# Graph attention on one core: the order of the seven block products of a pair of row tiles

## The chip, the core and the metric

The kernel runs on one core of a Trainium2 chip. TensorE (PE) does the matrix products into PSUM banks, VectorE (DVE), ScalarE (ACT) and GpSimd (POOL) do the elementwise work, and SyncE (SP), ACT and POOL issue the DMAs. The metric is the device time of one execution in microseconds (us). All data is float32. [...]

## The reference

```python
def reference(x, adj, W_q, b_q, W_k, b_k, W_v, b_v):   # x 2708 x 1024, adj 2708 x 2708
    h = maximum(layernorm(x, eps=1e-5), 0)
    q = h @ W_q.T + b_q;  k = h @ W_k.T + b_k;  v = h @ W_v.T + b_v
    z = (q @ k.T) / sqrt(1024) * adj
    z = where(z == 0, -10000, z)
    return x + relu(softmax(z, axis=1) @ v)
```

The entries of `adj` are 0 or 1, with about 4 ones in a row (probability 0.0014771 each). So a row attends to a handful of neighbours.

## The kernel before, in words

**What it computes.** The product of the query and key weights is formed once: M = W_q^T W_k with the scale, so that a score is (h_i M + c)·h_j. The rows of `h` go to DRAM (`h_dram`). A search finds up to 16 neighbours of every row. A counting sort orders the rows by their number of neighbours, so that a tile of 128 sorted rows needs only as many slots as its largest row; 21 full tiles are handled in this way, and 20 rows stay over. For every slot of a tile a gather fetches 128 neighbour rows (`g`); DVE multiplies them with the query rows and sums to one score a row (L664), ACT takes the exponential (L680), and DVE forms the weighted sum of the same rows (`weights`, then `sums` with L717). Each sum u is then multiplied by W_v, and relu, x and the scatter to the output follow. A general path at the end (from L1034) runs only for inputs that the sparse path can't handle.

**Seven products for a pair.** Two tiles of rows times a 1024 x 1024 matrix are eight block products of 128 x 512 x 512; `multiply` does them with seven, in the manner of Strassen and Winograd. `blocks` prepares the left operands: transposed quarters a11, a12, a22 (copied from PSUM by ACT) and their sums s1 to s4 (DVE, or partly POOL for the first pairs). `upper` transposes the first tile (8 transposes on PE), `lower` the second and forms the sums. The right operands are M's quarters and four sums of them in T. One block product is `add_block`: four matmuls that accumulate in one bank.

A pair uses three banks. X and Z are seeded with the bias by `banks_for` (two ACT copies), in the pair before. Y is a copy of X made by ACT (L789). In `multiply` the order is: X += a11·M00; Y = copy of X; Z += s1·T0; p5 = copy of Z; Y += s2·T1; u2 = copy of Y; X += a12·M10, and X is the first result c11; Y += s3·T2, then c22 = Y + p5 on DVE; Z += s4·M11, then c12 = Z + u2 on DVE; Y += a22·T3 and Y is the last result c21. A bank can be added to again only when its copy or sum has been read: Y·s3 waits for u2, Y·a22 for c22, Z·s4 for p5. Below, "Y·a22" means the product that adds a22·T3 to Y.

After each product `after(i)` with i from 0 to 6 runs other parts of the program: the next pair's `upper` at i = 0 and `lower` at i = 2 (for pair FIRST - 1 at 3 and 5), its bank seeds at 3, row loads, steps of the search, and a share of the attention.

**The units.** There are 20 units: ten query pairs (`q`, multiplied by M) and ten output pairs (`o`, multiplied by W_v), numbered n = 0 to 19. FIRST is 5: units 0 to 4 use the rows in their natural order, units 5 to 9 sorted rows. In between, M and T are loaded anew with W_v's blocks and sums (the loop at L981), each one after its last query product.

**What sets the order.** A scheduler in the framework orders each engine's instructions by its own estimate, except where the text says otherwise: ACT is in written order until the sort (`ordered`, closed at unit 2), and DVE is in written order from unit 5 on. `issue_after` keeps an instruction behind a named one. Each engine then executes its queue in order.

- `follow` runs the letters of `steps_at[(n, i)]`: `s` loads tiles of x and takes their statistics (`stats`), `r` takes the square root on ACT and six small DVE steps (`root`), `a` normalizes on ACT, stores to `h_dram` from POOL and adds to `hsum` on POOL (`apply`), `e` loads a tile of `adj` from SP, sums its rows on ACT (L260) and searches it on DVE (`edges`, four L263 and six small steps). Three buffers hold `adj` tiles.
- `searched` (at unit 2, i = 3) gives the buffers of the search back and loads W_v; `sort` (unit 2, i = 4) does the counting sort with two matmuls (L492, L494), the writing of the sorted table by 22 indirect DMAs of POOL (`put`) and the gathers of the first sorted rows; `ts_of_wv` forms the sums of W_v.
- `advance(share)` takes the next steps of the generator `attention` until about 2.8 us of DVE work are used up; it runs after each product, so the attention goes in step with PE. The list `chain` keeps DVE's attention in order, and `behind` holds DVE steps that later ones must follow.

Of the kernel before, what the change touches and what calls it, by code (L numbers as in the profile page):

```python
# [55 lines left out]
def tile_preln_masked_attention(  # L56
# [12 lines left out]
    nc = tc.nc  # L69
# [27 lines left out]
    tv_dram = dram.tile([4, P, 4, NB], FT, name="tv_dram")  # L97
# [76 lines left out]
    M = core.tile([P, 2, 2, 4, NB], FT, name="M")  # L174
# [34 lines left out]
    def root():  # L209

        group, xs, mv = normed.pop()
        G = len(group)
        mean, var = mv[:, :G, 0], mv[:, :G, 1]
        r = stat.tile([P, 5, 4], FT, tag="r", name="r")
        nc.scalar.activation(r[:, 0, :G], var, AF.Sqrt, bias=eps)
        nc.vector.reciprocal(r[:, 1, :G], r[:, 0, :G])
        nc.vector.scalar_tensor_tensor(r[:, 2, :G], var, EPS, r[:, 1, :G], op0=ALU.add, op1=ALU.mult)
        nc.vector.tensor_mul(r[:, 2, :G], r[:, 2, :G], r[:, 1, :G])
        nc.vector.tensor_scalar(r[:, 2, :G], r[:, 2, :G], -0.5, 1.5, op0=ALU.mult, op1=ALU.add)
        nc.vector.tensor_mul(r[:, 3, :G], r[:, 2, :G], r[:, 1, :G])  # L220
        last = nc.vector.scalar_tensor_tensor(r[:, 4, :G], mean, -1.0, r[:, 3, :G], op0=ALU.mult, op1=ALU.mult)
        normed.append((group, xs, r))
        if group[0] >= 16:
            roots.append(last)

    def apply():

        group, xs, r = normed.pop(0)
        for i, t in enumerate(group):
            t0, n = tiles[t]  # L230
            xt = xs[i]
            nc.scalar.activation(xt[:n], xt[:n], AF.Relu, bias=r[:n, 4, i:i + 1], scale=r[:n, 3, i:i + 1])  # L232
            nc.gpsimd.dma_start(h_dram[t0:t0 + n, :], xt[:n])  # L233
            nc.gpsimd.tensor_add(hsum[:n], hsum[:n], xt[:n])  # L234

    normed, adj_loads, roots = [], [], []

    def follow(steps):

# [82 lines left out]
    with tc.tile_pool(name="w", bufs=1, side="left") as wp:  # L322
# [83 lines left out]
        banks = []  # L406
# [8 lines left out]
    T = tp.tile([P, 4, 4, NB], FT, name="T")  # L415
    half = low.enter_context(tc.tile_pool(name="half", bufs=1, side="left", reuse_waits="tile"))

    def small(name):
        return half.tile([P, NB], FT, tag="half", name=name, bufs=14)
# [17 lines left out]
    FIRST = (EARLY - SINGLE) // 2  # L437
# [77 lines left out]
    behind = []  # L515
# [51 lines left out]
    ops_of = {0: blocks(*rows_of.pop(0), nc.gpsimd)}  # L567
    ops_of[0][1]()
    natural_rows(1)
    banks_of = {}  # L570
# [5 lines left out]
    q = query(hT.pop(0), banks, "e0", first=True, between=('e11 s16-17', ''), mid=open_first)  # L576
    nc.scalar.dma_start(q_dram[0:P, :], q)

    steps_at = {(0, 0): 'e12 r e13 a', (0, 3): 'e14 s18-19', (1, 0): 'e15 r e16 a', (1, 3): 'e17 s20-21 e18', (2, 0): 'r e19 a e20', (2, 2): 'e21'}
    
    slots, free = [], []

# [174 lines left out]
    done, held, at, ws, us = set(), {}, {}, {}, {}  # L757
# [20 lines left out]
    def add_block(bank, a, b, last=True):  # L778
        for c in range(4):
            mm = nc.tensor.matmul(bank, a[:, c, :], b[:, c, :], start=False, stop=(c == 3), skip_group_check=True)  # L780
        return mm

    def multiply(ops, banks, results, after, pause):


        X, Z = banks
        add_block(X, ops["a11"], M[:, 0, 0])
        Y = psum.tile([P, NB], FT, tag="acc", name="psy")
        nc.scalar.copy(Y, X)  # L789
        after(0)  # L790
        products.append(add_block(Z, ops["s1"], T[:, 0]))
        p5 = small("p5")
        nc.scalar.copy(p5, Z)
        after(1)
        add_block(Y, ops["s2"], T[:, 1])
        u2 = small("u2")
        nc.scalar.copy(u2, Y)
        after(2)
        add_block(X, ops["a12"], M[:, 1, 0])
        results[0](X)  # L800
        after(3)
        products.append(add_block(Y, ops["s3"], T[:, 2]))
        results[1](Y, p5)
        after(4)
        add_block(Z, ops["s4"], M[:, 1, 1])
        results[2](Z, u2)
        after(5)
        add_block(Y, ops["a22"], T[:, 3])
        results[3](Y)
        after(6)  # L810

    lo, hi = slice(0, NB), slice(NB, D)

    def q_results(ta, tb):
        qa = work.tile([P, D], FT, tag="q", name=f"q_{ta}", bufs=4)
        qb = work.tile([P, D], FT, tag="q", name=f"q_{tb}", bufs=4)

        def store(q, t):
            dst = q_dram[t * P:(t + 1) * P, :] if t < EARLY else q_late[(t - EARLY) * P:(t - EARLY + 1) * P, :]
            (nc.scalar if t < SINGLE + 2 * 2 else nc.sync).dma_start(dst, q)  # L820
            formed.add(t)

        def c11(X):
            nc.scalar.copy(qa[:, lo], X)

        def c22(Y, p5):
            nc.vector.tensor_add(qb[:, hi], Y, p5)  # L827

        def c12(Z, u2):
            behind.append(nc.vector.tensor_add(qa[:, hi], Z, u2))  # L830
            if ta >= EARLY:
                store(qa, ta)

        def c21(Y):
            nc.scalar.copy(qb[:, lo], Y)
            if ta < EARLY:
                store(qa, ta)
            store(qb, tb)

        return c11, c22, c12, c21  # L840
# [35 lines left out]
    def send(keep=0):  # L876
        while len(sent) > keep:
            y, t = sent.pop(0)
            scatter(y, t, P)
# [8 lines left out]
    def of_wv(i, j):  # L888

        return wv[j][:, i * 4:(i + 1) * 4, :]  # L890
# [22 lines left out]
    products = []  # L913
# [3 lines left out]
    def all_rows():  # L917
# [4 lines left out]
            nc.scalar.copy(hsum[:, h * NB:(h + 1) * NB], ps_h)  # L922
        summed.append(True)

    for n, unit in enumerate(units):
        kind, ta, tb = unit
        now[0] = n
        if n == FIRST:
            ordered.enter_context(tc.manual_schedule(engines={mybir.EngineType.DVE}))
        if FIRST - 1 <= n <= FIRST + 2:  # L930

            i, j = ((0, 0), (0, 1), (1, 0), (1, 1))[n - FIRST + 1]
            nc.sync.dma_start(m_dram[i, j], M[:, i, j])
        share = (20.0 if kind == "q" else 19.0) / 7
        nxt = units[n + 1] if n + 1 < len(units) else None
        results = (q_results if kind == "q" else o_results)(ta, tb)

        def after(i):
            if i in (2, 5):
                send()  # L940
            if (n, i) == (2, 4):
                with tc.issue_after(products[-1].ins):
                    placed.append(sort())
                ordered.close()
                ts_of_wv()
            if n == FIRST - 1 and i == 2:

                chain.append(behind[-1])
                next(stream)
            if n == FIRST - 1 and i == 6:  # L950
                chain.append(behind[-1])
            if n >= FIRST or n == FIRST - 1 and i == 6:
                advance(share)
            if nxt is not None:

                if i == (3 if n == FIRST - 1 else 0):
                    ops_of[n + 1] = blocks(*rows_of[n + 1], nc.gpsimd if n + 1 < FIRST - 1 else None)
                    ops_of[n + 1][1]()
                if i == (5 if n == FIRST - 1 else 2):
                    ops_of[n + 1][2]()  # L960
                    rows_of.pop(n + 1)
                    if n == last_q - 1:
                        all_rows()
                if i == 3:
                    banks_of[n + 1] = banks_for(bp_sb)
                if i == 2 and n + 2 < FIRST:
                    natural_rows(n + 2)
                if i == 4 and n + 2 >= FIRST and n + 2 < len(units) and n + 2 not in rows_of:
                    while units[n + 2][0] == "o" and not done.issuperset(units[n + 2][1:]):
                        advance(1.0)  # L970
                    rows_of[n + 2] = load_rows(units[n + 2])
            if (n, i) in steps_at:
                follow(steps_at[n, i])
            if (n, i) == (2, 3):
                searched()
            if n == last_q - 1 and i == 4:

                nc.sync.dma_start(bp_sb, bv.to_broadcast([P, D]))
                nc.vector.tensor_sub(bp_sb[:, NB:], bp_sb[:, NB:], bp_sb[:, :NB])

            for k, at in enumerate(((0, 0), (0, 2), (0, 4), (0, 6), (1, 0), (1, 2), (1, 3))):  # L981
                if (n - last_q, i) == at:
                    place, src = ((M[:, 0, 0], of_wv(0, 0)), (T[:, 0], tv_dram[0]), (T[:, 1], tv_dram[1]),
                                  (M[:, 1, 0], of_wv(1, 0)), (T[:, 2], tv_dram[2]), (M[:, 1, 1], of_wv(1, 1)),
                                  (T[:, 3], tv_dram[3]))[k]
                    nc.sync.dma_start(place, src)

        multiply(ops_of.pop(n)[0], banks_of.pop(n), results, after, None)
    ordered.close()
    send()  # L990
    while alone not in done:
# [25 lines left out]
    r, = load_rows(("o", alone))  # L1017
    uT = turned(r, "alone")
    X, Z = banks_for(bp_sb)
# [15 lines left out]
    with tc.If(some > 0):  # L1035
        with tc.tile_pool(name="big", bufs=1, side="right") as big, tc.tile_pool(
# [11 lines left out]
            for t, (t0, n) in enumerate(tiles):  # L1048
                ht = gen.tile([P, D], FT, tag="ht", name="g_h")
                nc.sync.dma_start(ht[:n], h_dram[t0:t0 + n, :])  # L1050
                for s in range(DC // 4):
                    pt = psum.tile([P, 4, P], FT, tag="tp", name="g_pt")
                    for c in range(4):
                        k = s * 4 + c
# [124 lines left out]
```

## Time and profile before

| what | value |
|---|---|
| median of 3 runs | 721.13 us (720.89 to 722.71) |
| profiled execution: its time | 724.53 us |
| profiled execution: span | 722.8 us |
| mean granted TensorE clock | 0.977 |
| DVE busy | 529.5 us (73%) |
| POOL busy | 358.8 us (50%) |
| ACT busy | 248.0 us (34%) |
| matmuls of L780, all forms | 1120 records |
| scores of L664 | 92, 1227 ns each |
| weighted sums of L717 | 77, 1283 ns each |
| searches of L263 | 88, 863 ns each |
| HBM read and written | 167.15 and 49.65 MB |

The span is the time from the first to the last instruction of the profiled execution; the execution's own time is 1.7 us longer, and 3.4 us above the median of the runs. A busy time is a sum over an engine's instructions. A bracket at the end of a line of a timeline tells how long the engine had been idle before it and what ended that. A product of `add_block` is eight records, since each float32 matmul is two. A name like ps, psy, a or s stands for all buffers of that name: ps for X and Z, psy for Y. POOL's times are rough.

### The profile page before, as it was taken

Reading aid. Unit: us, or ns where it says so; the run is one execution under the profiler, and the core shown is the slowest. Engines: PE = TensorE matmul, PEld = TensorE weight load, DVE = VectorE, ACT = ScalarE, POOL = GpSimd, SP = SyncE. Lnnn points to the kernel's source line nnn. Section 1 sums busy time; section 2 is a strip of 40 time slices with the busy share of each in tenths; the row PEclk is TensorE's granted clock in tenths of the full one; section 3 lists DMA queues with packets and bytes.
Section 4 is the critical chain, followed back from the end, with each engine's and each line's share of the span. In section 5 each row is a group of like instructions: output and inputs, shape, how many; then the busy total and the mean of one; then the engine's idle time right before and its main releaser. Section 6 shows DMA issues by size and latency. Waiting matters only on the chain. (4 is left out here: it accounts for less than half of the span.)

```text
span 722.8 us, 6371 instructions
## 1 busy us (share of the span) xinstructions
PE 680.3 (94%) x1796; PEld 347.4 (48%) x1796; DVE 529.5 (73%) x1053; ACT 248.0 (34%) x374; POOL 358.8 (50%) x310
## 2 busy tenths in 40 slices
PE   6999998998978999969999998999999989999995
PEld 4776775443433544424444443444444434444442
DVE  6989839986859820299989795989859979978301
ACT  0076177472834212223323212233323334322220
POOL 2066063241405457575666443565766876755341
PEclk9999999999989999998999999999999999999998
DMA  9998799998853672889989599989989799778652
GB/s 350 405 379 307 289 321 410 376 391 341 287 189 105 240 246 50 307 285 352 343 294 350 208 416 415 367 247 303 326 259 267 223 288 271 254 224 223 169 124 103
DMA packets 64453, 204.24 MB, mean 283 GB/s; under 512 B 9931, under 2 KB 10283, under 8 KB 63005
## 3 DMA queue, kind: packets, MB, share of 16 engines
q0 software_dynamic: 34592, 109.77, 46.6%
q1 hardware_dynamic: 27804, 87.19, 32.3%
q10 hardware_dynamic: 2016, 6.82, 2.4%
q8 instruction: 16, 0.26, 0.1%
q14 instruction: 25, 0.20, 0.1%
HBM read 167.15 MB, written 49.65 MB: 300 GB/s over the span
## 5 line engine op out<-in xcount | busy, mean ns | idle before, releaser
L432 POOL DMA_INDIRECT g<-h_dram,tab x106 | 129.4, 1221 | 54.0 <-issue 24.4
L780 PE MATMUL psy<-T,s 128*128 128x512 f32 x320 | 144.2, 593 | 5.6 <-ACT psy L789 3.2
L780 PE MATMUL ps<-M,a 128*128 128x512 f32 x320 | 144.2, 593 | 0.0
L664 DVE SCALAR_TENSOR_TENSOR junk<-g,pq 128x1024 uint8<-128x1024 f32 x92 | 112.8, 1227 | 28.9 <-DMA pq<-q_dram,tab 15.7
L359 PE MATMUL ps_m<-wk,wq 128*128 128x512 f32 x256 | 113.0, 604 | 5.5 <-DMA wk<-in_wk_dram 5.5
L717 DVE SCALAR_TENSOR_TENSOR u<-g,coef,u 128x1024 f32<-128x1024 f32 x77 | 98.8, 1283 | 12.5 <-ACT u L709 10.0
L780 PEld LDWEIGHTS psy<-T,s 128*128 128x128 f32 x320 | 60.5, 190 | 82.6 <-issue 73.8
L359 PEld LDWEIGHTS ps_m<-wk,wq 128*128 128x128 f32 x256 | 80.1, 314 | 36.4 <-DMA wk<-in_wk_dram 5.5
L780 PE MATMUL psy<-T,a 128*128 128x512 f32 x160 | 82.1, 660 | 15.2 <-DVE q L827 12.3
L780 PEld LDWEIGHTS ps<-M,a 128*128 128x128 f32 x320 | 59.6, 190 | 68.8 <-issue 68.8
L233 POOL DMA_DIRECT2D h_dram<-x x22 | 12.3, 561 | 127.0 <-ACT x L232 127.0
L263 DVE FIND_INDEX8 at<-ones,adj 128x8 uint32<-128x685 f32 (+1 forms) x88 | 75.0, 863 | 0.0
L780 PE MATMUL ps<-T,s 128*128 128x512 f32 x160 | 72.0, 593 | 0.0
L780 PE MATMUL ps<-M,s 128*128 128x512 f32 x160 | 71.9, 592 | 0.0
L780 PEld LDWEIGHTS psy<-T,a 128*128 128x128 f32 x160 | 33.4, 212 | 60.8 <-issue 40.5
L260 ACT ACTIVATE sized<-adj 128x2708 uint8<-128x2708 f32 (+1 forms) x22 | 54.2, 2462 | 2.2 <-DMA adj<-in_adj_dram 2.2
L618 POOL DMA_INDIRECT out_dram<-y,tab x21 | 24.5, 1168 | 59.2 <-DMA y<-in_x_dram,tab 58.3
L234 POOL TENSOR_TENSOR hsum<-hsum,x 128x1024 f32<-128x1024 f32 (+1 forms) x22 | 52.1, 2370 | 0.5
L780 PEld LDWEIGHTS ps<-M,s 128*128 128x128 f32 x160 | 30.4, 190 | 38.2 <-issue 38.2
L780 PEld LDWEIGHTS ps<-T,s 128*128 128x128 f32 x160 | 29.0, 190 | 29.6 <-issue 29.6
L845 POOL DMA_INDIRECT y<-in_x_dram,tab x21 | 35.1, 1673 | 14.5 <-DMA y<-tail_dram 5.2
L524 ACT COPY a<-pt 128x512 f32<-128x512 f32 x60 | 33.4, 591 | 6.8 <-PE pt L278 6.8
(193 smaller groups left out, 709.9 us busy)
## 6 DMA issues: line engine op xcount, KB each, us to landing
adj<-in_adj_dram SPq DMA_DIRECT2D x21, 1354.0 KB
x<-in_x_dram SPq DMA_DIRECT2D x21, 512.0 KB
h_dram<-x POOLq DMA_DIRECT2D x21, 512.0 KB
u_dram<-u POOLq DMA_DIRECT2D x15, 512.0 KB
or<-u_dram SPq DMA_DIRECT2D x15, 512.0 KB
h_e<-h_dram SPq DMA_DIRECT2D x11, 512.0 KB
q_late<-q SPq DMA_DIRECT2D x10, 512.0 KB
pq<-q_late POOLq DMA_DIRECT2D x10, 512.0 KB
```

The lines of the kernel that those rows point to most:

```text
L233: nc.gpsimd.dma_start(h_dram[t0:t0 + n, :], xt[:n])
L234: nc.gpsimd.tensor_add(hsum[:n], hsum[:n], xt[:n])
L260: nc.scalar.activation(sized[:n], a[:n, :, :PW], AF.Abs, accum_out=total[:n, t:t + 1])
L263: nc.vector.max_index(at[:n, g, :], ones[:n, 0:8], a[:n, g, :])
L359: nc.tensor.matmul(acc[i], lhs, wk_sb[o][:, cols], start=(o == 0), stop=(o == DC - 1))
L432: return nc.gpsimd.indirect_dma_start(out=dst, out_offset=None, in_=src, in_offset=off, bounds_check=N - 1, oob_is_err=False)
L524: nc.scalar.copy(ops[name], bank)
L618: to = nc.gpsimd.indirect_dma_start(out=out, out_offset=bass.IndirectOffsetOnAxis(ap=ptab.bitcast(U32)[:n, t, SLOTS:SLOTS + 1], axis=0), i ...
L664: chained(lambda: nc.vector.scalar_tensor_tensor(junk, g_of[t][s], 1.0, tq[t], op0=ALU.mult, op1=ALU.mult, accum_out=zall[:, t, s:s + 1]))
L717: chained(lambda: nc.vector.scalar_tensor_tensor(u, g_of[t][s], coef[:, at[t][s]:at[t][s] + 1], u, op0=ALU.mult, op1=ALU.add))
L780: mm = nc.tensor.matmul(bank, a[:, c, :], b[:, c, :], start=False, stop=(c == 3), skip_group_check=True)
L845: nc.gpsimd.indirect_dma_start(out=y[:n], out_offset=None, in_=x, in_offset=off, compute_op=ALU.add)
```

## The change

The order of the products changes, and some steps of the search stand elsewhere.

- A new function `opened(n)` does the first product of X and of Z of unit n. It is called for unit 0 ahead of the loop, and then in each unit between Y·s3 and Y·a22 for the next unit. In unit FIRST - 1 it is called after Y·a22.
- In `multiply` Z·s4 with c12 stands ahead of Y·s3 with c22. So the order is Y·s2, X·a12, Z·s4, Y·s3, X'·a11, Z'·s1, Y·a22, with a prime for the next unit. The copies to Y and to p5 stay at the start of `multiply`.
- c22 of query pairs goes into `behind`. The table's validity (`next(stream)`) is taken at i = 5 of unit FIRST - 1 instead of 2, `lower` there at 4 instead of 5, and the first share of `advance` falls in unit FIRST at i = 0.
- `steps_at` is rearranged: square roots go to the ends of units 0 and 1, normalizing follows at the next opening, and the last two tiles are searched from unit 2's opening. `searched` runs at i = 1 instead of 3 and `sort` at 3 instead of 4 of unit 2. A root becomes the barrier for later loads only when it is applied.
- The loads of W_v's blocks into M and T follow the new order of their last use.

```diff
         normed.append((group, xs, r))
+        last_of[group[0]] = last
+
+    def apply():
+
+        group, xs, r = normed.pop(0)
         if group[0] >= 16:
-            roots.append(last)
-
-    def apply():
-
-        group, xs, r = normed.pop(0)
+            roots.append(last_of[group[0]])
...
-    steps_at = {(0, 0): 'e12 r e13 a', (0, 3): 'e14 s18-19', (1, 0): 'e15 r e16 a', (1, 3): 'e17 s20-21 e18', (2, 0): 'r e19 a e20', (2, 2): 'e21'}
+    steps_at = {(0, 0): 'e12 r a e13', (0, 3): 'e14 s18-19 r e15', (1, 0): 'a e16 s20-21 e17', (1, 3): 'e18 r a e19', (2, 0): 'e20 e21'}
...
-    def multiply(ops, banks, results, after, pause):
-        X, Z = banks
-        add_block(X, ops["a11"], M[:, 0, 0])
+    def opened(n):
+        if n not in banks_of:
+            return
+        X, Z = banks_of[n]
+        ops = ops_of[n][0]
+        add_block(X, ops["a11"], M[:, 0, 0])
+        products.append(add_block(Z, ops["s1"], T[:, 0]))
+
+    def multiply(n, results, after):
+        X, Z = banks_of.pop(n)
+        ops = ops_of.pop(n)[0]
         Y = psum.tile([P, NB], FT, tag="acc", name="psy")
         nc.scalar.copy(Y, X)
         after(0)
-        products.append(add_block(Z, ops["s1"], T[:, 0]))
         p5 = small("p5")
         nc.scalar.copy(p5, Z)
         after(1)
-        add_block(Y, ops["s2"], T[:, 1])
+        products.append(add_block(Y, ops["s2"], T[:, 1]))
         u2 = small("u2")
         nc.scalar.copy(u2, Y)
         after(2)
         add_block(X, ops["a12"], M[:, 1, 0])
         results[0](X)
         after(3)
+        add_block(Z, ops["s4"], M[:, 1, 1])
+        results[2](Z, u2)
+        after(4)
         products.append(add_block(Y, ops["s3"], T[:, 2]))
         results[1](Y, p5)
-        after(4)
-        add_block(Z, ops["s4"], M[:, 1, 1])
-        results[2](Z, u2)
         after(5)
+        if n != FIRST - 1:
+            opened(n + 1)
         add_block(Y, ops["a22"], T[:, 3])
         results[3](Y)
+        if n == FIRST - 1:
+            opened(n + 1)
         after(6)
...
-            if (n, i) == (2, 4):
+            if (n, i) == (2, 3):
                 with tc.issue_after(products[-1].ins):
                     placed.append(sort())
...
-            if n == FIRST - 1 and i == 2:
+            if n == FIRST - 1 and i == 5:
                 chain.append(behind[-1])
                 next(stream)
...
-            if n >= FIRST or n == FIRST - 1 and i == 6:
+            if (n, i) >= (FIRST, 0):
                 advance(share)
...
-                if i == (5 if n == FIRST - 1 else 2):
+                if i == (4 if n == FIRST - 1 else 2):
                     ops_of[n + 1][2]()
...
-            if (n, i) == (2, 3):
+            if (n, i) == (2, 1):
                 searched()
...
-            for k, at in enumerate(((0, 0), (0, 2), (0, 4), (0, 6), (1, 0), (1, 2), (1, 3))):
+            for k, at in enumerate(((0, 0), (0, 1), (0, 3), (0, 4), (0, 5), (0, 6), (1, 2))):
```

## The prediction

> **What bounds the kernel now.** I read the page first, then TensorE's (PE's) own waits, then the timelines of PE, ACT and DVE around each wait.
>
> ```profile
> PE 680.3 (94%) x1796; PEld 347.4 (48%) x1796; DVE 529.5 (73%) x1053; ACT 248.0 (34%) x374; POOL 358.8 (50%) x310
> ```
>
> PE works in 94% of the span. So only its holes can be won, and any delay of a product is paid in full. The waits of PE by what ended them, in us in total, number, longest:
>
> ```profile
> PE psy L780 <- DVE q L827: 12.3, 5, 4.0
> PE psy L780 <- ACT psy L789: 3.2, 1, 3.2
> PE ps_in L492 <- DVE hot L488: 3.0, 1, 3.0
> PE psy L780 <- DVE p L855: 2.7, 1, 2.7
> PE psy L780 <- ACT u L797: 2.3, 2, 2.1
> ```
>
> All five stand in the code that changes. Together with the small remainders they are 23.6 us: the last product of a pair, Y·a22, waits for the DVE addition c22 that reads its bank (15.0 us in six waits, rows L827 and L855); three products wait for an ACT copy (5.6); the sort's product waits for the searches (3.0). Two further rows, a weight load at the start (5.5) and a seed copy of the first query (4.1), are untouched. PE's timeline shows what a wait costs behind itself:
>
> ```profile
> 163.62 3.60 PE L780 MATMUL ps<-M,s 128*128 128x512 f32 x8
> 169.43 5.40 PE L780 MATMUL psy<-T,a 128*128 128x512 f32 x8 [2.21 <-DVE q L827]
> 202.91 6.17 PE L780 MATMUL psy<-T,a 128*128 128x512 f32 x8 [4.02 <-DVE q L827]
> 311.60 3.70 PE L780 MATMUL psy<-T,s 128*128 128x512 f32 x8 [2.10 <-ACT u L797]
> 324.88 6.63 PE L780 MATMUL psy<-T,a 128*128 128x512 f32 x8 [3.58 <-DVE q L827]
> ```
>
> A product takes 3.44 us from start to start, but 5.23 to 6.47 after some waits. The windows of PE give the reason (us, PE busy, granted clock, DMA share, GB/s):
>
> ```profile
> 171.00:173.00 2.00, 2.00 (x4) 0.50 1.07 415
> 445.00:447.00 2.00, 2.00 (x5) 1.00 0.99 410
> ```
>
> After the 2.21 us wait the clock is 0.50; after a 3.24 us wait (444.8) it is 1.00. Over all waits of the touched stretch the next start minus 3.44 sums to 11.6 us: 1.8 + 2.6 + 0.3 + 1.7 (sort) + 3.0 + 1.8, and 0.1 four times. So 23.6 + 11.6 = 35.2 us can be won at most.
>
> Why are the additions late?
>
> ```profile
> 182.53 0.17 DVE L216 RECIPROCAL r<-r 128x2 f32<-128x2 f32 x1 [7.96 <-ACT r L215]
> 202.20 0.66 DVE L827 TENSOR_TENSOR q<-psy,p 128x512 f32<-128x512 f32 x1
> 307.06 1.23 DVE L664 SCALAR_TENSOR_TENSOR junk<-g,pq 128x1024 uint8<-128x1024 f32 x1 [13.65 <-DMA pq<-q_dram,tab]
> 444.03 0.21 ACT L680 ACTIVATE w<-zall 128x6 f32<-128x6 f32 x1 [9.61 <-DVE junk L664]
> 444.14 0.58 ACT L789 COPY psy<-ps 128x512 f32<-128x512 f32 x1
> ```
>
> DVE idles 8 us because the square root r stands late in ACT's fixed order, then has the searches of that stretch in front of c22 (202.20). The attention stream begins only when the last query rows are gathered (307.06) and then runs ahead of c22 in pair 5. At 444 a copy that PE needs sits in ACT's queue behind an exponential that waits for DVE.
>
> **The change, part by part.** No arithmetic is added: PE keeps 140 products in the pairs. What moves is order; I follow the instruction order of the built changed kernel with durations of the rows above.
>
> *Y·a22.* Now X·a11 and Z·s1 of the next pair stand between Y·s3 and Y·a22, so c22 has 6.9 us instead of 3.4. Removed: the five DVE waits, 15.0 us, and their slow clock, 9.6, except where DVE is later than that. The exception is pair 4 (the last natural pair): only one matmul, 0.86 us, stands between; c22 ends 0.25 + 0.69 + 0.1 = 1.05 after Y·s3: 0.2 to 0.3 us left instead of 2.2.
>
> *u2 and the Y copy.* u2 has two products, and the copy of X into Y has Z·s1, Y·a22 and eight transposes (7.7 us instead of 4.3). In the scheduled part of ACT the copy at unit 10 now stands ahead of the exponential. Removed: 5.6 us and 0.3 of clock.
>
> *Steps moved forward.* The roots go from the openings of pairs 1 and 2 to the end of pairs 0 and 1, the searches of tiles 20 and 21 from (2,2) to (2,0), the sort from (2,4) to (2,3). Their row loads and table loads go with them on SP's queue. There the two rows of pair 4 now stand ahead of the load of tile 19; it would wait for ACT's pass over tile 16 anyway, until 188.3 (187.7 before), so SP costs nothing. POOL's store and hsum of 18 to 21 move with the apply step; the two-operand DVE steps beside them stretch (L265, 0.19 us alone, 1.56 to 2.17 beside L234), so I give DVE 2 to 3 us per pair for that.
>
> Now the waits that come in. In pairs 0 and 1 ACT runs in written order.
> - Pair 0. The transposes of the next rows stand behind Z·s1, so ACT's copies of them end at 153.4 instead of 149.8; behind them: a row sum 2.45, the root, six DVE steps 1.3, two applies 2.4, a second row sum 2.45, then p5 at 162.5 to 163.0. Z·s4 comes a product earlier, at 161.1, and overwrites what p5 reads: 2.0 us of wait, and 0.9 for a slow clock in half of such cases. After this c22 ends at 177.1, wanted at 176.9: 0.3.
> - The copy into the next Y stands behind the copy of Y·a22 and two DMA issues on ACT (0.9 us, row at 174.87): 0.2 + 0.5 + 0.95 + 0.6 less the transposes' 0.87 and overlap leaves 1.0, twice: 2.0.
> - Pair 1: p5 behind two row sums, 0.9. Pair 2: p5 behind the last sums and the sort's product, 0.4. The searches end near 213 (231 before) and the sort's positions stand near 225 (242.5 before); c22 of pair 2, now behind nine subtractions of 0.64, ends at 231.4, wanted at 232.5.
> - Pair 5. Call E the end of Y·a22 of pair 4 (293.85 before). DVE's first score came at E+13.2. POOL's gathers (all of its chain moves with the sort) are now out before E, so the stores of pair 4's queries don't queue behind them; the bounds are E+13.2 and E+7; I take E+10. Behind it stand eight scores, the s block, two sums and c12: 19.1, so c22 ends at E+29.1, wanted at E+28.4: 0.7 (0 to 4).
> - Unit 10, the new place of an old wait. c22 of unit 9 to the coefficients took 17.7 us (426.96 to 444.7) with 6.8 us of waits for gathers. With Y·a22 starting at R, c22 is now at R-6.7, coefficients at R+11.0; ACT then does the weighted row 1.15, c21 0.5, two copies 1.0 and p5: R+14.4, while Z·s4 is ready at R+12.0: 2.4, with 0.9 for the clock. The seven weight loads of that place (1 MB each) are asked for in some 28 us instead of 36, at a DMA share of 1.02: the bounds are 0 and 6.
> - Unit 16: c22 now stands behind the coefficients of an edgeless tile; both come to about 17.1 us after the transposes: 0 to 2, I take 1.
> - Elsewhere: s1 is wanted 13.7 us after its transposes instead of 18, bank seeds 6.9 after they are asked for. No row shows such waits; the bounds are 0 (all is ready) and 8 (one short wait in half the pairs). I take 3, near the small waits that the trace has (0.25, 0.41).
>
> Left or new: 2.9 + 0.3 + 2.0 + 0.9 + 0.4 + 0.3 + 0.7 + 3.3 + 1.0 + 3.0 = 14.8. Gain: 35.2 - 14.8 = 20.4. The tail (PE's end at 714.3 to 722.8) is untouched: the last pair's Y·a22 is covered by the transposes of the tile that is left alone.
>
> **A rule against the trace.** The Trainium skill, TensorE: Matmul & The Clock Gate, Part 1, says that PE drops to half rate after an idle window of about 3.4 us and needs as long a busy one to return, and that the window is free-running. By it only the waits of 4.02 and 3.58 us would have cost clock: 5.6 of the 11.6 us, and my 2.0 and 2.4 us waits nothing: 29.2 - 13.0 = 16.2, 704.9 us. The rows show half rate after 2.21 and 2.69 and full rate after 3.24, so length alone doesn't decide. I use the measured 11.6 and half of 1.8 for a new wait of two us.
>
> **The sum.** The profiled execution took 724.5 us (span 722.8), 3.4 above the median of 721.1. The gain lies in waits that this execution shows; I take it off the median: 721.1 - 20.4 = 700.7.
>
> **Rivals.**
> - *Waits only change places* (0.19): DVE stays as late as it was (pair 5 keeps 4 us and its clock, 7), early ACT waits and unit 10 reach their upper ends (12 and 6). For it: 38 us of ACT's waits are for L664. Against it: DVE has 8 us holes twice that the moved roots fill. 712 (709 to 718).
> - *Nearly all gone* (0.05): DVE is early enough everywhere, only pair 0 and the Y copies wait: 689.
> - *Slower, p5 becomes the bound* (0.06): the copy p5 stands on ACT behind exponential and weighted row, which wait for DVE; it ends 3.4 us after the coefficients. It decides from coefficients later than R+8.6 in a unit. If all 15 attention units had them at R+11.5, that is 2.9 us each, 43 us in all: 721.1 - 35.2 + 43 = 729. For it: unit 10. Against it: only there do gathers come this late; most units have 3 to 7 scores, not 15.
> - That the change doesn't reach PE's order is excluded but for pair 4: the built order has the two products between.
>
> **Numbers.** Likeliest (0.70): 700.7, its own range 692 to 709 (6 to 23 us left). The range of 691 to 714 leaves out most of the second, the upper half of the first rival and the third. A measurement of this kernel can tell about 0.3% (2.2 us) from no change: faster 0.93, same 0.02, slower 0.05.
>
> **What would show it.** Right: no L780 wait of PE for the c22 addition over 1 us beyond pair 5, square-root holes on DVE under 6 us, the sort's positions 13 or more us earlier, a short wait of Z·s4 for p5 in pairs 0 and 10, PE clock at 0.9 or more in nearly all slices. Wrong: waits for p5 in many units, waits for s1 or for weights (DMA into M or T), or a sort no earlier.

## The result, and the profile after

The changed kernel takes 711.9 us (median) against 721.9 us for the kernel before in the same series: ratio 0.987, interval 0.983 to 0.991, so 10.0 us faster. The forecast was 20.4 us. The two profiled executions lie 12.6 us apart: span 722.8 before and 710.2 after, granted clock 0.977 and 0.987. The one of the kernel before took 2.6 us more than its median, the one of the changed kernel 0.2.

PE's waits after, apart from three idle times ahead of the pairs (5.5, 3.7 and 0.8 us), by what ended them (total us, number, longest):

```profile
PE psy L781 <- DVE p L869: 11.9, 3, 7.5
PE ps L781 <- ACT p L802: 2.2, 2, 1.4
PE psy L781 <- ACT psy L799: 1.8, 2, 0.9
PE pt L279 <- DMA qr<-h_dram,tab: 1.6, 1, 1.6
PE psy L781 <- DVE q L841: 1.4, 2, 0.9
```

The line numbers have moved: L781 is the product, L841 and L869 are the addition c22 of the query and of the output pairs. The c22 waits of the query pairs fell from 12.3 to 1.4 us and the sort's wait of 3.0 is gone, but c22 of the output pairs rose from 2.7 to 11.9. PE's timeline says where:

```profile
311.20 3.70 PE L781 MATMUL psy<-T,a 128*128 128x512 f32 x8 [0.91 <-DVE q L841]
316.47 1.06 PE L279 MATMUL pt<-ident,qr 128*128 128x128 f32 x8 [1.57 <-DMA qr<-h_dram,tab]
554.77 5.71 PE L781 MATMUL psy<-T,a 128*128 128x512 f32 x8 [7.54 <-DVE p L869]
586.61 5.15 PE L781 MATMUL psy<-T,a 128*128 128x512 f32 x8 [4.00 <-DVE p L869]
```

Between 317 and 554 us PE has no wait of 0.3 us or more. Then two products wait for c22, Y·a22 of unit 14 (554.77) and of unit 15 (586.61), and each is slow afterwards. The window behind the first (us, PE busy, PEld, DVE, ACT, POOL, granted clock, DMA share, GB/s):

```profile
556.00:558.00 2.00, 2.00 (x3) 0.79 (x3) 1.93 (x5) 1.15 (x1) 1.70 (x2) 0.50 0.04 2
```

The two waits and their slow clock (2.1 and 1.6 us) are 15.2 us. Pair 4's Y·a22 now ends at 281.8 instead of 293.9 us: 12.1 us are won by then, and from there to the end of the span both kernels need the same (428.9 and 428.4). So the question is why c22 is late at 554 and 586, and where the rest of the forecast gain, 20.4 - 12.1 = 8.3 us behind pair 4, went.

### The profile page after: what moved, and what is told of

The parts are those of the page before. It is cut to its first block, busy times and chain, and to the rows that moved or that the text cites. A ratio compares the mean times of both kernels' runs of the same rounds, so it can differ in the third digit from the quotient of the medians.

```text
span 710.2 us, 6368 instructions
## 1 busy us (share of the span) xinstructions
PE 672.7 (95%) x1796; PEld 344.8 (49%) x1796; DVE 527.5 (74%) x1053; ACT 246.6 (35%) x374; POOL 356.2 (50%) x309
## 5 line engine op out<-in xcount | busy, mean ns | idle before, releaser
L433 POOL DMA_INDIRECT g<-h_dram,tab x106 | 127.1, 1199 | 46.8 <-issue 24.8
L781 PE MATMUL psy<-T,s 128*128 128x512 f32 x320 | 144.0, 593 | 1.8 <-ACT psy L799 1.8
L781 PE MATMUL ps<-M,a 128*128 128x512 f32 x320 | 144.0, 592 | 0.0
L781 PEld LDWEIGHTS ps<-M,a 128*128 128x128 f32 x320 | 59.6, 190 | 69.4 <-issue 69.4
L781 PEld LDWEIGHTS psy<-T,s 128*128 128x128 f32 x320 | 59.3, 190 | 69.6 <-issue 69.4
L781 PE MATMUL psy<-T,a 128*128 128x512 f32 x160 | 76.0, 620 | 13.3 <-DVE p L869 11.9
L781 PE MATMUL ps<-M,s 128*128 128x512 f32 x160 | 72.2, 593 | 2.2 <-ACT p L802 2.2
L781 PE MATMUL ps<-T,s 128*128 128x512 f32 x160 | 71.9, 592 | 0.0
L619 POOL DMA_INDIRECT out_dram<-y,tab x21 | 25.0, 1192 | 92.5 <-DMA y<-in_x_dram,tab 88.1
L781 PEld LDWEIGHTS psy<-T,a 128*128 128x128 f32 x160 | 31.2, 199 | 54.6 <-issue 36.5
L781 PEld LDWEIGHTS ps<-M,s 128*128 128x128 f32 x160 | 30.1, 190 | 39.3 <-issue 35.9
L781 PEld LDWEIGHTS ps<-T,s 128*128 128x128 f32 x160 | 30.4, 190 | 38.3 <-issue 37.8
L710 ACT ACTIVATE u<-g,coef 128x1024 f32<-128x1024 f32 x19 | 21.9, 1151 | 47.2 <-DVE coef L709 37.2
L859 POOL DMA_INDIRECT y<-in_x_dram,tab x21 | 34.7, 1651 | 6.4 <-issue 5.2
```

The costliest lines, as they stand in the source:

```text
L433: return nc.gpsimd.indirect_dma_start(out=dst, out_offset=None, in_=src, in_offset=off, bounds_check=N - 1, oob_is_err=False)
L619: to = nc.gpsimd.indirect_dma_start(out=out, out_offset=bass.IndirectOffsetOnAxis(ap=ptab.bitcast(U32)[:n, t, SLOTS:SLOTS + 1], axis=0), i ...
L710: nc.scalar.activation(u, g_of[t][0], AF.Copy, scale=coef[:, at[t][0]:at[t][0] + 1])
L859: nc.gpsimd.indirect_dma_start(out=y[:n], out_offset=None, in_=x, in_offset=off, compute_op=ALU.add)
```

## What POOL does there

DVE's waits for transfers ahead of its scores, and POOL's waits at the output scatter, between 440 and 690 us; first the kernel before, then the changed one:

```profile
DVE junk L664 <- DMA g<-h_dram,tab: 6.2, 3, 4.7
DVE junk L664 <- DMA M<-h_dram,tab: 3.8, 2, 2.5
POOL out_dram L618 <- DMA y<-in_x_dram,tab: 55.5, 16, 8.4
```

```profile
DVE junk L665 <- DMA g<-h_dram,tab: 17.3, 12, 3.0
DVE junk L665 <- DMA M<-h_dram,tab: 4.1, 2, 3.8
POOL out_dram L619 <- DMA y<-in_x_dram,tab: 83.9, 18, 9.8
```

With the query rows pq, DVE waits 14.2 us for transfers before and 29.4 after. An output row tile needs two DMAs of POOL: `add_x` adds the rows of x to y in SBUF (L845 before, L859 after), then `scatter` writes y to its rows of the output (L618, L619), and POOL waits at the scatter until the add has landed, as the brackets below show. The Trainium skill, DMA: Bandwidth & Descriptors, section "Two DMAs through the same engine are not ordered", gives the reason for the wait: sharing a queue doesn't order a DMA behind one that it depends on, so the issuing engine has to wait for the first one's semaphore. The same stretch of POOL's timeline, before:

```profile
520.86 1.59 POOL L845 DMA_INDIRECT y<-in_x_dram,tab  x1 [0.31 <-issue]
522.75 2.15 POOL L845 DMA_INDIRECT y<-in_x_dram,tab  x1 [0.30 <-issue]
525.21 1.68 POOL L432 DMA_INDIRECT g<-h_dram,tab  x1 [0.30 <-issue]
529.28 1.19 POOL L618 DMA_INDIRECT out_dram<-y,tab  x1 [2.39 <-DMA y<-in_x_dram,tab]
533.47 0.97 POOL L618 DMA_INDIRECT out_dram<-y,tab  x1 [3.00 <-DMA y<-in_x_dram,tab]
```

and after:

```profile
515.05 1.59 POOL L859 DMA_INDIRECT y<-in_x_dram,tab  x1 [0.30 <-issue]
...
525.22 0.99 POOL L619 DMA_INDIRECT out_dram<-y,tab  x1 [5.63 <-DMA y<-in_x_dram,tab]
526.51 1.40 POOL L433 DMA_INDIRECT g<-h_dram,tab  x1 [0.30 <-issue]
528.22 1.57 POOL L859 DMA_INDIRECT y<-in_x_dram,tab  x1 [0.31 <-issue]
529.23 1.19 POOL L642 DMA_DIRECT2D pq<-q_late  x1
535.29 1.68 POOL L619 DMA_INDIRECT out_dram<-y,tab  x1 [4.86 <-DMA y<-in_x_dram,tab]
537.27 1.53 POOL L433 DMA_INDIRECT g<-h_dram,tab  x1 [0.30 <-issue]
```

Before, c12 and c21 are one product apart (3.4 us), and the scheduler put both adds ahead of both scatters in seven of the nine pairs of this stretch: one stretch of waiting a pair. After, Z·s4 stands ahead of Y·s3, and X'·a11 and Z'·s1 stand ahead of Y·a22, so c21's bank is complete four products after c12's: each add gets its own scatter and its own wait, and in these rows no later gather passes it. The gather issued at 537.27 stood behind the wait of 4.86. The next score on DVE that waited for gathered rows came at 542.73; c12 and c22 of unit 14 stood behind it, and PE's Y·a22 waited for this c22:

```profile
542.73 1.23 DVE L665 SCALAR_TENSOR_TENSOR junk<-g,pq 128x1024 uint8<-128x1024 f32 x1 [2.97 <-DMA g<-h_dram,tab]
554.03 0.69 DVE L869 TENSOR_TENSOR p<-psy,p 128x512 f32<-128x512 f32 x1
```

From 542.73 on DVE is busy nearly all the time until c22, with scores and sums that stand in front of it. So these rows allow two readings, too much work in front of c22 or rows that come too late. The experiments decide.

## The experiments

Ratios are to the kernel before in the same series, with 95% intervals; its median was 718 to 722 us, so ratios compare across series and times do so only roughly. The theories: **A**, the step at i == 4 that forces out the attention sums needed by unit n + 2 now stands between c12 and c22, and its four sums (5.24 us) delay c22. **B**, the waits at the scatters hold back the gathers. **C**, the dropped first share of `advance` makes the stream late. **D**, DVE's own work sets the pace. **E**, the transfers are slow, whoever waits.

**The forcing step and the share.** The edits of the first three, on the changed kernel:

```diff
-                if i == 4 and n + 2 >= FIRST and n + 2 < len(units) and n + 2 not in rows_of:
+                if i == 5 and n + 2 >= FIRST and n + 2 < len(units) and n + 2 not in rows_of:
```

```diff
-            if (n, i) >= (FIRST, 0):
+            if n >= FIRST or n == FIRST - 1 and i == 6:
```

> The changed kernel with one edit: the step that forces out the attention sums of unit n+2 and loads its rows stands at i == 5, behind c22, instead of i == 4, between c12 and c22. Theory A (that step stands in front of c22): in the unit where Y·a22 waited 7.54 us, four sums (5.24 us) and one score (1.2 us) leave the front of c22, so at most 1.1 us of the wait and nothing of its 2.1 us of slow clock stay; the 4.00 us wait one unit and a half later (1.55 us of clock) goes too or at least halves, since the edgeless tile's weights no longer stand in front of c22. Sum 10 to 14 us: 698 to 702 us. Theory B (DVE is late because gathers land late behind scatters on POOL's queue): the place of the step changes little, c22 still waits behind scores for late gathers, 707 to 712 us.

Measured: 712.8 us, 0.988 (0.984 to 0.991), as the change itself. The two waits stayed and only changed sizes (the profiled execution took 717.1 us, 4.3 above the median; it also has a wait of 3.16 us in pair 5):

```profile
553.87 5.17 PE L781 MATMUL psy<-T,a 128*128 128x512 f32 x8 [3.66 <-DVE p L869]
588.53 6.60 PE L781 MATMUL psy<-T,a 128*128 128x512 f32 x8 [7.14 <-DVE p L869]
```

> The changed kernel with one edit: the attention stream gets back its first share of time, at (FIRST-1, 6), so that it runs 2.86 us ahead of where it is in the changed kernel. Theory A: the four sums still stand between c12 and c22 in the same unit (only five small weight steps, 0.6 us, leave that place), so the 7.54 us wait shrinks by no more than 3 us: 708 to 712 us. Theory C (the dropped share made the stream late): both waits go, 698 to 703 us.

Measured: 715.3 us, 0.993 (0.990 to 0.996).

> Both edits: the forcing step at i == 5 and the first share restored. Theory A: as the forcing step alone, within 2 us of it, 697 to 702 us. Theory C: the same as the share alone. Theory B: 706 to 712 us.

Measured: 714.6 us, 0.991 (0.988 to 0.994), a little above B's 706 to 712 us. Theory A's edit applied to the kernel before (i == 3 for i == 4):

> The kernel before with one edit: the forcing step at i == 3, ahead of c22, instead of i == 4, behind it. In the kernel before, c22 at 562.20 is followed directly by four sums of 5.24 us, and Y·a22 starts 0.05 us after c22, without slack. Theory A: those sums and a score (1.3 us) now stand in front of c22, a wait of 5 to 6.5 us and 2 us of slow clock come in there, of which the following wait of 2.69 us may give some back: slower than before by 3 to 8 us. Theory B: within 2 us of the kernel before.

Measured: 720.9 us, 1.000 (0.996 to 1.003). So A and C fall: what is taken from the front of c22 in one place is late in another.

**Scatters and DVE's work, first attempt.** The place of `send` alone, on the changed kernel, then on the kernel before, and with the step at i == 5:

```diff
-            if i in (2, 5):
-                send()
+            if i in (4, 6):
+                send(keep=1)
```

> The changed kernel, forcing step untouched; only the place of the output scatters on POOL's queue moves: each is issued two products later (at i == 4 and i == 6, keeping back the row tile whose x was just asked for), so that c21's scatter has again the distance from its add of x that it has in the kernel before. Theory B (in the changed kernel the scatter of c21 stands 6.9 us nearer to its add of x, POOL waits 62 instead of 39 us for these adds between 295 and 640 us, and the gathers behind them reach DVE late): POOL's scatter waits fall to 40 us or less, DVE's gather waits halve, the two PE waits of 7.5 and 4.0 us shrink to under 4 us together: 700 to 706 us. Theory D (DVE's own work sets the pace in the attention stretch): scatter waits fall as well, but c22 is as late as before, 710 to 714 us.

Measured: 710.2 us, 0.984 (0.980 to 0.989). The scatter waits did not fall:

```profile
POOL out_dram L619 <- DMA y<-in_x_dram,tab: 85.4, 18, 10.3
```

They are 85.4 us between 440 and 690: the adds still stand apart, and at most four other DMAs stand between an add and its scatter in the rows from 480 to 600. So this run didn't test B, nor did its counterpart on the kernel before (i in (0, 5)), where these waits hardly rose (58.1 us for 55.5):

> The kernel before with c21's scatters issued two products sooner (at i == 0 instead of 2), which gives them the short distance that they have in the changed kernel. Theory B: POOL's scatter waits rise from 39 to near 60 us between 295 and 640 us, gathers are late, c22 of two or three late units waits longer: 3 to 8 us slower than before. Theory D: within 2 us of before.

Measured: 722.4 us, 1.001 (0.997 to 1.005).

> The changed kernel with the later scatters and the forcing step at i == 5 behind c22. If late gathers (B) and the four sums in front of c22 (A) each cost part of the 15 us, neither edit alone frees them and both do: 696 to 701 us. By D it stays at 709 to 714 us.

Measured: 710.9 us, 0.986 (0.981 to 0.992); the scatter waits were still 74.7 us, so this run tests B as little. The run against D leaves the last sum of a tile out of the result (`if s < K[t] - 1 or K[t] < 4:` ahead of it):

> The changed kernel without the last attention sum of every tile of four or more edges (left out of the result; its gather and its place in the stream stay): DVE loses some 20 instructions of 1.31 us, about 14 of them ahead of the wait at 554.8. Theory D: the two waits at 554.8 and 586.6 go, with their clock 15 us: 695 to 700 us. Theory B: gathers land as before, c22 only loses what DVE did between late gathers: 703 to 710 us.

Measured: 719.7 us, 1.000 (0.996 to 1.004), slower than the changed kernel, though DVE is busy 511.1 us instead of 527.5. D falls; B's 703 to 710 us did not come either. DVE with less work waits longer for gathered rows; the same view as above:

```profile
DVE junk L665 <- DMA g<-h_dram,tab: 24.1, 15, 4.5
DVE junk L665 <- DMA pq<-q_late: 8.5, 2, 5.4
DVE junk L665 <- DMA M<-h_dram,tab: 6.9, 4, 2.7
```

The trace shows where the 7.8 us between the two spans lie. 2.9 stand ahead of the end of PE's last product: c22 waits of 4.31 and 4.24 us in units 13 and 14 and a copy wait of 3.39 us, each with a slow product behind it. 4.9 stand in the tail after it: the last scatter leaves POOL at 710.5 instead of 702.7 us, behind two others that waited for their adds. Why the waits moved to these units isn't shown.

**Scatter k after add k + 1.** Now the wait itself is taken away: by the time of the next add the one before has landed.

```diff
...
-    def send(keep=0):
+    def send(keep=1):
         while len(sent) > keep:
             y, t = sent.pop(0)
-            scatter(y, t, P)
+            with tc.issue_after(adds[len(outs) + 1].ins) if keep else nullcontext():
+                scatter(y, t, P)
...
```

(`add_x` now notes its adds in the list `adds`, and the call behind the last unit is `send(keep=0)`.)

> The changed kernel; each output scatter is issued on POOL only after the next row tile's add of x (so add k+1, then scatter k), nothing else. Between 440 and 690 us POOL's scatters waited for their adds 55 us in the kernel before, where the adds of a pair stand together and share one wait, and 84 us in the changed kernel, where each add is followed by its own scatter. Theory B (these waits hold back the gathers behind them, so DVE's stream and with it c22 is late): the scatter waits fall under 15 us, DVE's waits for gathers (18.2 + 8.2 us between 295 and 640) to under 14, the PE waits at 554.8 and 586.6 from 11.5 to under 4 us: 698 to 704 us. Theory E (the transfers themselves are slow, whoever waits): the scatter waits go, gathers land as late as before, 707 to 712 us.

Measured: 696.6 us, 0.971 (0.968 to 0.974). The scatter waits between 440 and 690, and all PE waits of this kernel over the whole span:

```profile
POOL out_dram L619 <- DMA y<-in_x_dram,tab: 4.5, 3, 2.6
```

```profile
PE ps_m L360 <- DMA wq<-in_wq_dram: 5.6, 1, 5.6
PE ps L313 <- ACT ps L295: 3.8, 1, 3.8
PE psy L781 <- DVE q L841: 2.3, 2, 1.8
PE ps L781 <- ACT p L802: 2.1, 2, 1.4
PE psy L781 <- ACT psy L799: 1.8, 2, 0.9
PE pt L279 <- DMA qr<-h_dram,tab: 1.7, 1, 1.7
```

No c22 wait of an output pair is left, though the four sums still stand in front of c22, and DVE has no wait for g, M or pq in that stretch (29.4 us in the changed kernel). It is a little faster than B's 698 to 704 us. B holds and E falls.

> As the one before, with the forcing step at i == 5, behind c22. If DVE is then early (B) the four sums in front of c22 matter little: within 3 us of the one before. If DVE stays about 4 us late, the five instructions that leave the front of c22 count now: 3 to 6 us faster than the one before. Theory E: 707 to 712 us.

Measured: 695.6 us, 0.970 (0.967 to 0.973), the same as without the moved step.

> The changed kernel with scatter k after add k+1, the forcing step behind c22, and the stream's first share restored. Theory B with a stream 2.86 us earlier: no PE wait over 2 us between 330 and 690 us, 697 to 702 us; in the earlier pairs the added scores ahead of c22 of pair 5 cost up to 3 us. Theory E: 708 to 714 us.

Measured: 698.2 us, 0.972 (0.969 to 0.975); c22 of pair 5 waits 2.85 us instead of 1.26, which the earlier stream costs.

> The kernel before with the same place of the scatters (scatter k after add k+1). Its scatter waits are 55 us between 440 and 690, and only one PE wait stands there (2.69 us at 592.2, 1.8 us of clock). Theory B: that wait shrinks or goes, 0 to 5 us faster than before, so much less than the same edit brings in the changed kernel. Theory E: within 2 us of before.

Measured: 718.9 us, 1.001 (0.998 to 1.004). Its profile lacks the c22 wait of 2.69 us, but the time can't be told from before: as long as the adds stand in pairs, the scatter waits cost too little to be told. Part of what it wins goes into the tail behind PE's last product, which is 9.7 us here for 8.5 before.

**Adds apart in the kernel before.** The converse:

```diff
     def add_x(y, t, n=P):
         ...
-        nc.gpsimd.indirect_dma_start(out=y[:n], ..., compute_op=ALU.add)
+        with tc.issue_after(outs[-1].ins) if outs else nullcontext():
+            nc.gpsimd.indirect_dma_start(out=y[:n], ..., compute_op=ALU.add)
```

> The kernel before, with each add of x issued on POOL only after the scatter before it, so that a pair's adds no longer stand together; nothing else. Theory B: POOL's scatter waits rise from 55 to about 80 us between 440 and 690, DVE's waits for gathers double, c22 is late in two or three more pairs: 5 to 15 us slower than before. If separated adds are not enough (the products' new order is needed as well): within 3 us of before.

Measured: 733.8 us, 1.015 (1.007 to 1.024). Slower by 12 us, with the lines (the last one over the whole span)

```profile
DVE junk L664 <- DMA M<-h_dram,tab: 12.3, 6, 5.9
DVE junk L664 <- DMA g<-h_dram,tab: 11.5, 5, 5.0
POOL out_dram L618 <- DMA y<-in_x_dram,tab: 62.9, 16, 8.1
PE psy L780 <- DVE p L856: 8.0, 3, 4.1
```

DVE's waits doubled as expected (27.8 with pq); POOL's rose only from 55.5 to 62.9, not to 80, so the total of POOL's waits is not the measure; that it counts which gathers stand behind them is a reading that no run tests alone. PE waits for c22 of output pairs three times (8.0 us) instead of once (2.7). Adds apart are enough to make DVE late, without the new product order. Not all of the loss is DVE's: of the 10.2 us between the two spans 6.9 come before the end of PE's last product and 3.3 in the tail behind it, where each add now waits for the scatter ahead of it.

**The parts.** The search part alone is the diff's lines on `roots`, `steps_at`, `searched` and `sort`; the order alone is the rest.

> The kernel before with the change's search part alone: roots at the end of pairs 0 and 1, tiles 20 and 21 at (2, 0), the searched positions at (2, 1), the sort at (2, 3); products in their old order. The forecast counted the c22 wait of pair 1 (4.02 us and its clock), the sort's wait (2.97 and its clock) and part of the waits for the stream's start to this part. If both parts work alone: 5 to 9 us faster. If the searches only help together with the new order (c22 still has one product of slack): within 3 us of before.

Measured: 705.9 us, 0.977 (0.969 to 0.985): 15.8 us faster, about twice the expected. What is left in its PE timeline, of 0.3 us or more, is only

```profile
171.68 5.40 PE L781 MATMUL psy<-T,a 128*128 128x512 f32 x8 [4.02 <-DVE q L828]
308.57 5.40 PE L781 MATMUL psy<-T,a 128*128 128x512 f32 x8 [3.57 <-DVE q L828]
427.48 5.40 PE L781 MATMUL psy<-T,s 128*128 128x512 f32 x8 [3.49 <-ACT psy L790]
575.81 5.12 PE L781 MATMUL psy<-T,a 128*128 128x512 f32 x8 [2.84 <-DVE p L856]
```

The waits of pair 1 (4.02), pair 4 (2.10), the sort (2.97) and the copy at 311 (2.10) are gone without any second product of slack; that of pair 0 grew from 2.21 to 4.02.

> The changed kernel with the search steps at their old places, so the products' order alone. The adds of x stand apart here too, so theory B expects long waits of Y·a22 near 550 to 590 us, as in the changed kernel: what is won before 300 us is given back there, 713 to 720 us. If the search part is what brings the gain, it is 718 us or more.

Measured: 725.4 us, 1.005 (1.001 to 1.009), slower than before; Y·a22 waits 7.27 us at 568.1 and 4.18 at 600.0.

> The products' order alone (searches at their old places) with scatter k issued after add k+1. Theory B: no long wait after 330 us; only the early waits that the search part removes stay, 5 to 9 us above the changed kernel with the same scatters (696.6): 701 to 706 us.

Measured: 708.1 us, 0.982 (0.975 to 0.989), somewhat more than expected; no wait of 0.3 us or more after the one at 325 us.

> The kernel before with the search steps of the change and scatter k after add k+1, products in their old order. If the products' order is worth its removed waits once the scatters are out of the way, this lies 6 to 9 us above the kernel that has all three (696.6): 702 to 706 us, about what the search steps alone gave (705.9), since the only wait that the scatters can still remove is 2.8 us. If the order is worth nothing, 695 to 699 us.

Measured: 705.0 us, 0.979 (0.973 to 0.985), as expected if the order is worth its removed waits. The eight corners, as ratios to the kernel before:

| | searches old | searches moved |
|---|---|---|
| products old, scatters old | 1 | 0.977 |
| products new, scatters old | 1.005 | 0.987 (the change) |
| products old, scatter k after add k + 1 | 1.001 | 0.979 |
| products new, scatter k after add k + 1 | 0.982 | 0.971 |

With the old scatters the new order costs 0.5 to 1.0%; with the scatters out of the way it brings 1.9% without and 0.8% with the moved searches. The corners come from different series and neighbouring intervals touch (0.969 to 0.985 for the searches alone, 0.983 to 0.991 for the change), so the steps are middle values; but as far as they tell, the moved searches alone brought at least as much as the whole change. The two corners with old products and new scatters carry a longer tail (9.7 and 10.0 us for 8.5), so the new scatters look a little worse there than they are for the pairs.

**p5 on ACT.** Row sums e13 and e17 moved to (0, 1) and (1, 1), behind p5, on the fastest version:

> All three (search steps, products' order, scatter k after add k+1) with the forcing step behind c22, and the row sum e13 moved from the end of step (0, 0) to (0, 1), e17 from (1, 0) to (1, 1), so that on ACT the copy p5 stands ahead of them. The waits of Z·s4 for p5 (1.35 and 0.78 us) should go, c22 of pair 0 (0.57) is not later: 1 to 2.5 us faster than the same kernel without it (695.6), 693 to 695 us. If the row sums are then late for the roots behind them, the sort moves and it is no faster.

Measured: 697.0 us, 0.967 (0.961 to 0.973). The two p5 waits went, but c22 of pair 0 waits 3.01 us instead of 0.57: no gain that can be told, and the wait changed its place.

The fastest kernels of the study, at 695.6 to 697.0 us, can't be told apart.

## Why the prediction was right and wrong

- **The waits that go** (35.2 us to win): right in kind. The c22 waits of the query pairs and the sort's fell from 15.3 us to under 2; pair 4's fell from 2.10 to nothing; unit 10's copy wait (3.24) is gone. The runs put more of this on the searches than the text did, which credited the second product of slack.
- **The early waits that come in**: right. p5 in pair 0: 1.36 for 2.0; c22 there 0.53 for 0.3; the Y copies 0.86 and 0.91 for 1.0 each; p5 in pair 1: 0.80 for 0.9; pair 5: 0.91 for 0.7. The clock stayed at full rate behind all of them, so the 0.9 for a slow one in pair 0 didn't come. The sort's positions end at 225.7, forecast near 225. DVE's wait for the square root is 5.3 us at 155.7 and not visible in the other two places (under 6 was forecast).
- **Unit 10** (3.3 forecast): nothing came; p5 was not late.
- **Elsewhere** (3.0): one wait of 1.57 for gathered query rows at 316.5.
- **Unit 16** (0 to 2, taken as 1): here lies the step that failed. The forecast took off all c22 waits and their clock "except where DVE is later than that", and for the output pairs this item was the only exception. By the rows, the coefficients of the edgeless tile (of `EMPTY` in the kernel) stand in front of c22 of unit 15, not of unit 16:

```profile
584.14 0.17 DVE L695 TENSOR_SCALAR coef<-keys 128x2 f32<-128x2 f32 x1
585.87 0.68 DVE L869 TENSOR_TENSOR p<-psy,p 128x512 f32<-128x512 f32 x1
```

Unit 15 waited 4.00 us, and unit 14, for which there was no term at all, 7.54; unit 16 waited 0.32. So the forecast's own sign of being right, no c22 wait over 1 us beyond pair 5, failed. With their clock the two are 15.2 us. This step looked at DVE's queue only: how many of DVE's instructions stand in front of c22. It took for granted that the rows for the scores are there as early as before. c12 and c21 each issue two DMAs on POOL, and moving their products apart broke up the pairs of adds; the text's own list of what a moved step issues left these out. With that one thing mended both waits are gone: all waits of 0.3 us or more in the touched stretch are then 7.9 us, and the kernel is 21.7 us faster than the kernel before of its series, near the forecast of 20.4. That it comes so near is in part luck, since unit 10 and the small waits were put too high.
- **The sum.** Term by term 22.5 us are left for the 14.8 of the forecast: 4.5 for 6.5 in pairs 0 to 2, 0.9 for 1.0 in pairs 4 and 5, nothing for 3.3 in unit 10, 15.5 for 1.0 in units 14 to 16, 1.6 for 3.0 elsewhere. 35.2 - 22.5 = 12.7, and the spans differ by 12.6. The medians differ by 10.0 only: the forecast took the waits of an execution that lay 3.4 us above the median (2.6 above that of the later series) for those of the median.
- **The rivals.** "Waits only change places", at 712, gave the right time by luck, for other reasons: it had 4 us and clock left in pair 5 and long ACT waits early and in unit 10, and none of these came at that size. None of the rivals was late gathers. "p5 becomes the bound" didn't appear.
- **The clock rule.** Length alone doesn't decide: across these runs products took 5.4 us for 3.7 behind waits of 2.20, 2.69 and 2.83 us and ran at full rate behind waits of 2.25, 2.95, 3.24 and 3.60. The Trainium skill (TensorE: Matmul & The Clock Gate, Part 1) lets the clock drop after an idle window of about 3.4 us and calls the window free-running. That would allow full rate after 3.60 us, but not half rate after 2.20; the measurement decides, and no run here shows the window itself. Half of the clock cost for a wait of about 2 us was too much: of the waits between 1.9 and 2.5 us that stand ahead of a product in these profiles, four were followed by a slow one, all four the same product near 169 us, and twelve by one at full rate. In the changed kernel it weighed little, as the wait of 2.0 came out at 1.36.

## What to carry to other kernels

When products are moved, follow each result past its reading engine to the DMAs that it issues, and look at what shares that queue: an issuing engine that waits for one transfer to land delays the gathers of other work behind it (POOL's waits here: 83.9 us between 440 and 690, and 4.5 once they were moved). Put a dependent DMA behind the next independent one, so that its wait is over when its turn comes. Try the parts of a change by themselves: here one part brought at least as much as the whole, and the other's cost lay in a queue that its diff doesn't mention.

## What was not expected of the hardware

- An indirect add of 512 KB and the scatter behind it stood 6.5 to 11.4 us apart in the changed kernel between 440 and 690 us (issue to issue, 18 pairs), also where nothing stood between them (7.7 us at 488.2 to 496.0); POOL waited 1.7 to 9.8 us of it.
- Less DVE work did not shorten the changed kernel at all: with 16 us less of it the time rose to that of the kernel before, with DVE's waits for transfers up from 29.4 to 39.5 us between 440 and 690 us and a tail that was 4.9 us longer.
